# A graph layer on one core: more columns of x[src] on two engines, and their registers loaded eight at a time

## The chip, the core and the metric

One Trainium2 chip, one of its cores. A core has five engines that run their own instruction streams side by side: TensorE (PE; its weight loads are listed as PEld), VectorE (DVE), ScalarE (ACT), GpSimd (POOL) and SyncE (SP, which here only issues transfers). Each engine has a sequencer that takes the instructions in order, does some of them itself (register loads, waits, issuing DMAs) and hands the others on to the engine. The metric is the device time of one execution in microseconds (us), the median of several runs.

## What is computed

A message-passing layer over 12,500 nodes of 64 features and 400,000 edges, sorted by `dst`, with 16 features an edge, followed by a residual and a layer norm. All is float32.

```
m_in = concatenate([x[src], x[dst], edge_attr])      # 400000 x 144
h = silu(m_in @ W1 + b1)
messages = silu(h @ W2 + b2)
agg = segment_sum(messages, dst)                     # 12500 x 64
x = layernorm(x + silu(concatenate([x, agg]) @ W3 + b3))
```

## The kernel before

**Tiles.** 128 edges are a tile, eight tiles an octet; there are 391 octets. Two tiles that lie side by side are a pair (256 edges, four pairs an octet). The loop over octets (`for o in range(NO + 1)`, L601) has a fixed order of instructions on TensorE, ScalarE, VectorE and SyncE (`manual_schedule`, L598): an engine meets its instructions in the order in which the loop body writes them.

**An octet.** `first_layer` (L434) multiplies `xw` (the window's part of the first layer, with the weights of the edge features) by `oh` on L441, and adds the part of `x[src]`. ScalarE takes the silu into `h` (L458). `second_layer` (L461), an octet later, multiplies by W2 (L469), and ScalarE takes the second silu into `m` (L473). `add_up` (L476) sums messages by node with `eh` as a matrix of zeros and ones (L482), and VectorE adds the sums to `agg` (L487). VectorE also builds `oh` by a compare (L424), copies `xw` out of PSUM (L402), and builds `eh` by another compare (L430).

**Where x[src] comes from.** Three ways, side by side:

- *Gathers.* GpSimd issues one indirect DMA a tile (L373), 128 rows of `pa = x @ W1[:64]`, three octets ahead, into one of five tiles `ga`. TensorE adds them through `ident` (L454).
- *Columns.* For some octets the first pair isn't gathered. Instead it is put together, column by column, from `xs`, a copy of x transposed that lies in SBUF. Each edge is one instruction: 64 partitions of 4 bytes are copied from a place given by a register, by ScalarE with a copy (L299), by VectorE with a reduction over one element (L297). TensorE multiplies the finished tile `cx` by `w1d` (L451). The index row of a pair is fetched by SyncE (L351, three octets ahead of the pair's first column), and made into addresses by VectorE (L359).
- *Rows.* Now and then the second pair isn't gathered either: SyncE copies 16 rows an octet, each with a DMA of its own (L324).

**How columns are dealt out.** `columns(o, engine, part)` (L271) is called four times an octet: for VectorE ahead of `first_layer` (L642, behind the compare of L424) and behind `compare_nodes` (L650, behind `xw` and `eh`); for ScalarE ahead of the first silu (L456) and ahead of the second (L471). `ACOLS` and `VCOLS` (L31, L32) say how many columns a call does: 32 and 28 on ScalarE, 32 and 32 on VectorE. `RATE` (L261) is their sum, 124 an octet, so a pair of 256 takes 2.06 octets and there are 182 such pairs. A call works in pieces. Each piece first loads its addresses from the index row into registers (L290, one load instruction for the whole piece), then does its columns. `LOADS` (L34) sets the size of a piece: up to 16 for the first of a call and up to 8 for the others, fewer at the end of a call or where a tile of 128 ends.

Of the kernel before, what the change touches and what calls it, by code (L numbers as in the profile page):

```python
# [20 lines left out]
P = 128  # L21
# [6 lines left out]
AHEAD = 3  # L28
RAW = 12
TABLES = 7  # L30
ACOLS = (32, 28)  # L31
VCOLS = (32, 32)  # L32
ROWS = 16
LOADS = (16, 8)  # L34
XBASE = (0, 64 << 18)
XADDR = 36864
LAG = CT * P // 32
# [60 lines left out]
def windows(ctx, tc, ident, badi, pa, x, xt, src_c, src_row, dst_c, dst_row, attr_t, dst_2, attr_2, base, w1, b1, w2, b2, w3, b3, out, edges):  # L98
    nc = tc.nc
    N, D = x.shape  # L100
# [55 lines left out]
    for s in range(3):  # L156
        part = const.tile([1, D], BF16, name=f"part{s}")
# [90 lines left out]
    with tc.tile_pool(name="gat", bufs=AHEAD + 2) as gat, tc.tile_pool(name="drp", bufs=2) as drp, \  # L248
# [11 lines left out]

        RATE = sum(ACOLS) + sum(VCOLS)  # L261
        pairs = []
        while True:
            o = RAW + -(-2 * P * (len(pairs) + 1) // RATE) + 1
# [3 lines left out]
        cols, indices = {}, {}  # L268
        xb = xs.bitcast(U8)

        def columns(o, eng, part):  # L271
            if o < RAW:
                return
            lo = (o - RAW) * RATE
            if eng == ENG.Activation:
                lo, n = lo + sum(ACOLS[:part]), ACOLS[part]
            else:
                lo, n = lo + sum(ACOLS) + sum(VCOLS[:part]), VCOLS[part]
            hi, todo = lo + n, n
            while lo < hi:  # L280
                j, e0 = lo // (2 * P), lo % (2 * P)
                if j >= len(pairs):
                    return
                n = min(hi - lo, P - e0 % P, LOADS[lo > hi - todo])
                if pairs[j] not in cols:
                    cols[pairs[j]] = cx.tile([P, P], F32, name="cx")
                t = cols[pairs[j]].bitcast(U8)
                s = e0 // P
                h = slice(s * D, (s + 1) * D)
                _, regs = nc.values_load_multi_w_load_instructions(  # L290
                    indices[j][0:1, e0:e0 + n], engines=(eng,), min_val=XBASE[s] + XADDR,
                    max_val=XBASE[s] + XADDR + 4 * (N - 1), skip_runtime_bounds_check_because="src names a node")
                for e, r in zip(range(e0 % P, e0 % P + n), regs):
                    to, frm = t[h, 4 * e:4 * e + 4], xb[h, ds(r - (XBASE[s] + XADDR), 4)]
                    if eng == ENG.DVE:

                        nc.vector.tensor_reduce(to, frm[:, :, None], AX.X, OP.max)  # L297
                    else:
                        nc.scalar.copy(to, frm)  # L299
                lo += n  # L300


        rpairs = []
        while True:
            o = RAW + -(-2 * P * (len(rpairs) + 1) // ROWS) + 1
# [128 lines left out]
        def first_layer(o):  # L434
            c, t0, n, first, last = octs[o]
            n2 = n + n % 2
            k = n2 // 2
            ga = got.pop(o)
            oh, eh = hots.pop(o)
            p1 = ps1.tile([P, OT // 2, P], F32, name="p1")  # L440
            nc.tensor.matmul(p1[:, :k], xw[o % 3], oh, start=True, stop=False, skip_group_check=True)  # L441
            if o < RAW:
                pt = mis.tile([P, OT // 2, P], F32, name="mm")
                for i in range(k):
                    nc.tensor.matmul(pt[:, i, :], ga[:, 2 * i:2 * i + 2, :].rearrange("p s d -> p (s d)"), ident,  # L445
                                     start=True, stop=True)
                xg = work.tile([P, OT // 2, P], F32, name="m")
                nc.vector.tensor_copy(xg[:, :k], pt[:, :k])
                nc.tensor.matmul(p1[:, :k], w1d, xg[:, :k], start=False, stop=True, skip_group_check=True)
            if o in pairs:  # L450
                nc.tensor.matmul(p1[:, 0, :], w1d, cols.pop(o), start=False, stop=False, skip_group_check=True)  # L451
            for i in range(1 if o in pairs else 0, k if o >= RAW else 0):
                g2 = single.pop(o) if o in rpairs and i == 1 else ga[:, 2 * i:2 * i + 2, :]
                nc.tensor.matmul(p1[:, i, :], g2.rearrange("p s d -> p (s d)"), ident,  # L454
                                 start=False, stop=(i == k - 1), skip_group_check=True)
            columns(o, ENG.Activation, 0)  # L456
            h = work.tile([P, OT // 2, P], F32, name="h")
            nc.scalar.activation(h[:, :k], p1[:, :k], AF.Silu, bias=b1s)  # L458
            made[o] = h, eh

        def second_layer(o):  # L461
            c, t0, n, first, last = octs[o]
            n2 = n + n % 2
            k = n2 // 2
            h, eh = made.pop(o)
            p2 = ps2.tile([P, OT, D], F32, name="p2")
            nc.tensor.matmul(p2[:, :n2, :], one3, b2r[:, :n2, :], start=True, stop=False, skip_group_check=True)  # L467
            for i in range(k):
                nc.tensor.matmul(p2[:, 2 * i:2 * i + 2, :].rearrange("p s d -> p (s d)"), h[:, i, :], w2d,  # L469
                                 start=False, stop=(i == k - 1), skip_group_check=True)  # L470
            columns(o + 1, ENG.Activation, 1)  # L471
            m = work.tile([P, OT, D], F32, name="m")
            nc.scalar.activation(m[:, :n2], p2[:, :n2], AF.Silu)  # L473
            made[o] = m, eh
# [85 lines left out]
        todo = {}  # L560
# [7 lines left out]
        for q in range(early):  # L568
            o = lead[due[q]] + 3 if q < rest else NO
# [4 lines left out]
        for q0, q1 in batches:  # L574
            o = lead[due[q1 - 1]] + 3
# [22 lines left out]
        with tc.manual_schedule(engines={ENG.PE, ENG.Activation, ENG.DVE, ENG.SP}):  # L598
            compare_dst(0)
            compare_nodes(0)  # L600
            for o in range(NO + 1):  # L601
# [3 lines left out]
                for k in parts[3 * o - 3:3 * o] if o else []:  # L605
                    n = min(XC, NP - k)
# [33 lines left out]
                if o + 1 < NO:  # L640
                    compare_dst(o + 1)
                columns(o, ENG.DVE, 0)  # L642
                if o < NO:
                    first_layer(o)
# [10 lines left out]
                if 30 <= o < 30 + 2 * LP and o % 2 == 0:  # L655
                    k = (o - 30) // 2
                    part = rel[:, k * TILES // LP:(k + 1) * TILES // LP]
# [307 lines left out]
```

## Time and profile before

| What | Number |
|---|---|
| time, median of 3 runs | 5,184.74 us (5,167.56 to 5,185.11) |
| the profiled execution | 5,200.1 us, of which the span is 5,197.9 us |
| TensorE busy | 2,932.5 us (56%) |
| VectorE busy | 2,641.3 us (51%) |
| ScalarE busy | 2,906.1 us (56%) |
| GpSimd busy | 2,565.3 us (49%) |
| mean granted clock of TensorE | 0.629 |
| a column on VectorE (L297) | 150 ns, 24,032 times |
| a column on ScalarE (L299) | 188 ns, 22,560 times |
| a gather (L373) | 944 ns, 2,619 times from `pa` |
| compare `oh` (L424), `eh` (L430), copy `xw` (L402) | 674, 545, 282 ns |
| silu `h` (L458), silu `m` (L473) | 684, 593 ns |

No engine is busy much over half of the span. The busy shares are flat over the span from its third slice of 40 on, so that one octet is like another: 5,198 us over 391 octets are 13.3 us each. The durations of consecutive columns overlap, so a run of them takes less than their number times the mean. Register loads are done by the sequencer and count as idle time of the engine; so does a wait that the profile can't put down to another instruction, which it calls "issue". A letter q behind an engine's name marks what its sequencer does.

### The profile page before, as it was taken

How to read it: one execution, taken by the hardware profiler on the slowest of the kernel's cores; microseconds unless marked ns; L12 is line 12 of the kernel's file. 1: busy time of each engine (PE TensorE's matmuls, PEld its weight loads, DVE VectorE, ACT ScalarE, POOL GpSimd, SP SyncE). 2: the span in 40 equal slices, each digit the busy share in tenths (PEclk: the TensorE clock that was granted, in tenths of full speed). 3: DMA queues.
4: the chain of work that ended last, by engine and by line, in shares of the span. 5: the costliest groups of instructions: out<-in, count | busy, mean ns of one | idle time of the engine just before them, and what ended most of it. 6: DMA issues, size and time to landing. Idle time of an engine off the chain costs nothing. (4 is left out here: it accounts for less than half of the span.)

```text
span 5197.9 us, 107486 instructions
## 1 busy us (share of the span) xinstructions
PE 2932.5 (56%) x15131; PEld 2075.4 (40%) x15131; DVE 2641.3 (51%) x26395; ACT 2906.1 (56%) x23402; POOL 2565.3 (49%) x2724
## 2 busy tenths in 40 slices
PE   5655655555555555555564655656555555555566
PEld 3443434434433344343343434434433343344344
DVE  1255555545555555555555555555555555555555
ACT  1255555555555655655556565555556555655555
POOL 5544454454444544445444444545454444555453
PEclk7666565666666666666656566565656666665656
DMA  4321111211211121122112211211211221121121
GB/s 85 86 46 39 40 39 40 47 39 40 46 42 43 40 46 40 40 43 42 41 40 49 43 40 42 44 39 40 47 40 40 44 47 40 40 47 39 40 46 40
DMA packets 203943, 229.98 MB, mean 44 GB/s; under 512 B 133612, under 2 KB 141988, under 8 KB 202324
## 3 DMA queue, kind: packets, MB, share of 16 engines
q1 hardware_dynamic: 101528, 122.61, 10.5%
q0 software_dynamic: 86880, 89.14, 9.1%
q10 hardware_dynamic: 14812, 11.26, 0.9%
q14 instruction: 595, 4.87, 0.3%
q8 instruction: 128, 2.10, 0.2%
HBM read 216.36 MB, written 6.40 MB: 43 GB/s over the span
## 5 line engine op out<-in xcount | busy, mean ns | idle before, releaser
L373 POOL DMA_INDIRECT ga<-pa,sc x2619 | 2472.2, 944 | 2516.1 <-PE p L454 1699.8
L299 ACT COPY cx<-xs 64x4 uint8 x22560 | 2404.2, 188 | 1406.1 <-issue 1362.4
L297 DVE TENSOR_REDUCE cx<-xs 64x4 uint8 x24032 | 1910.3, 150 | 1806.6 <-issue 1740.9
L441 PE MATMUL p<-oh,xw 128*128 128x512 f32 (+1 forms) x782 | 772.4, 1089 | 1529.3 <-DVE xw L402 727.6
L441 PEld LDWEIGHTS p<-oh,xw 128*128 128x128 f32 x782 | 187.1, 297 | 1637.1 <-DVE xw L402 776.3
L482 PE MATMUL pg<-eh,m 128*64 128x48 f32 x6250 | 363.0, 277 | 588.6 <-ACT m L473 174.1
L454 PEld LDWEIGHTS p<-ident,ga 128*128 128x128 f32 x2620 | 591.3, 314 | 194.9 <-issue 193.6
L469 PE MATMUL p<-w2d,h 128*128 128x128 f32 x3126 | 642.0, 369 | 1.5 <-issue 1.4
L469 PEld LDWEIGHTS p<-w2d,h 128*128 128x128 f32 x3126 | 545.3, 263 | 133.0 <-issue 133.0
L454 PE MATMUL p<-ident,ga 128*128 128x128 f32 x2620 | 593.2, 397 | 0.0
L482 PEld LDWEIGHTS pg<-eh,m 128*64 128x64 f32 x6250 | 312.1, 189 | 680.2 <-issue 342.2
L473 ACT ACTIVATE m<-p 128x512 f32<-128x512 f32 x391 | 231.8, 593 | 474.9 <-remote 308.9
L458 ACT ACTIVATE h<-p,b1s 128x512 f32<-128x512 f32 x391 | 267.4, 684 | 319.0 <-remote 138.6
L402 DVE TENSOR_TENSOR xw<-mm,mask 96x128 f32<-96x128 f32 x391 | 110.4, 282 | 439.9 <-issue 392.4
L397 PE MATMUL mm<-w1bb,xr 64*96 64x128 f32 x782 | 241.0, 401 | 72.6 <-ACT z L523 49.9
L424 DVE TENSOR_TENSOR oh<-dr,wrow 96x512 f32<-96x512 int32 x391 | 263.6, 674 | 6.3 <-issue 3.5
L430 DVE TENSOR_TENSOR eh<-wrow,dc 128x384 f32<-128x384 f32 x391 | 213.2, 545 | 42.2 <-issue 42.2
L467 PE MATMUL p<-b2r,one 3*128 3x512 bf16 x391 | 194.5, 498 | 0.0
L451 PEld LDWEIGHTS p<-cx,w1d 128*128 128x128 f32 x364 | 116.0, 319 | 175.4 <-issue 175.4
L397 PEld LDWEIGHTS mm<-w1bb,xr 64*96 64x96 f32 x782 | 127.8, 214 | 144.7 <-issue 68.7
L487 DVE TENSOR_TENSOR agg<-agg,pg 128x48 f32 x391 | 77.3, 198 | 123.4 <-remote 32.3
L373 POOL DMA_INDIRECT ga<-in_x,sc x96 | 91.0, 948 | 63.5 <-PE mm L445 28.9
(81 smaller groups left out, 802.7 us busy)
## 6 DMA issues: line engine op xcount, KB each, us to landing
rx<-pa SPq DMA_DIRECT2D x5888, 0.2 KB
dr<-in_dst SPq DMA_DIRECT2D x260, 288.0 KB
ga<-pa,sc POOLq DMA_INDIRECT x2619
oh<-in_attr SPq DMA_DIRECT2D x130, 192.0 KB
xr<-in_xt SPq DMA_DIRECT2D x391, 24.0 KB
xs<-in_xt ACTq DMA_DIRECT2D x12, 512.0 KB
pa<-v ACTq DMA_DIRECT2D x12, 256.0 KB
xa<-in_x SPq DMA_DIRECT2D x24, 128.0 KB
```

Source lines behind the costliest of these rows:

```text
L297: nc.vector.tensor_reduce(to, frm[:, :, None], AX.X, OP.max)
L299: nc.scalar.copy(to, frm)
L373: nc.gpsimd.indirect_dma_start(out=ga[:, i, :], out_offset=None, in_=x if o < RAW else pa[:, :], in_offset=bass.IndirectOffsetOnAxis(ap=sc ...
L397: nc.tensor.matmul(pw[:E, :], winrow[o].rearrange("k s w -> k (s w)"), w1bb.rearrange("k s m -> k (s m)"), start=True, stop=True)
L424: nc.vector.tensor_tensor(oh[:E, :], dr[:, e:e + w], wn[:E, o:o + 1].to_broadcast([E, w]), op=OP.is_equal)
L430: nc.vector.tensor_tensor(eh[:, :n], row[:, None, :].to_broadcast([P, n, S]), rel[:, t0:t0 + n, None].to_broadcast([P, n, S]), op=OP.is_equal)
L441: nc.tensor.matmul(p1[:, :k], xw[o % 3], oh, start=True, stop=False, skip_group_check=True)
L454: nc.tensor.matmul(p1[:, i, :], g2.rearrange("p s d -> p (s d)"), ident, start=False, stop=(i == k - 1), skip_group_check=True)
L458: nc.scalar.activation(h[:, :k], p1[:, :k], AF.Silu, bias=b1s)
L469: nc.tensor.matmul(p2[:, 2 * i:2 * i + 2, :].rearrange("p s d -> p (s d)"), h[:, i, :], w2d, start=False, stop=(i == k - 1), skip_group_ch ...
L473: nc.scalar.activation(m[:, :n2], p2[:, :n2], AF.Silu)
L482: nc.tensor.matmul(pg[s * D:(s + 1) * D, :], m[:, i, :], eh[:, i, :], start=(i < 2), stop=(i >= n - 2), skip_group_check=True)
```

## The change

Each of the two engines does 68 columns an octet: 36 in the first call and 32 in the second. `RATE` becomes 136, a pair takes 1.88 octets, and there are 199 pairs by columns. Every piece has at most eight columns, the first of a call too. `columns` is cut into three functions: `pieces` yields the sizes, `addresses` loads the registers, `columns` calls both. The loads stay where they were in the order of each engine: right ahead of the columns that use them. The calls of `columns` are the same four, at the same places.

```diff
-ACOLS = (32, 28)
-VCOLS = (32, 32)
+ACOLS = (36, 32)
+VCOLS = (36, 32)
 ROWS = 16
-LOADS = (16, 8)
+LOADS = 8
...
-        def columns(o, eng, part):
+        def pieces(o, eng, part):
...
-            hi, todo = lo + n, n
+            hi = lo + n
             while lo < hi:
                 j, e0 = lo // (2 * P), lo % (2 * P)
                 if j >= len(pairs):
                     return
-                n = min(hi - lo, P - e0 % P, LOADS[lo > hi - todo])
+                n = min(hi - lo, P - e0 % P, LOADS)
+                yield j, e0, n
+                lo += n
+
+        def addresses(eng, j, e0, n):
+            s = e0 // P
+            _, regs = nc.values_load_multi_w_load_instructions(
+                indices[j][0:1, e0:e0 + n], engines=(eng,), min_val=XBASE[s] + XADDR,
+                max_val=XBASE[s] + XADDR + 4 * (N - 1), skip_runtime_bounds_check_because="src names a node")
+            return regs
+
+        def columns(o, eng, part):
+            for j, e0, n in pieces(o, eng, part):
+                regs = addresses(eng, j, e0, n)
                 if pairs[j] not in cols:
                     cols[pairs[j]] = cx.tile([P, P], F32, name="cx")
                 t = cols[pairs[j]].bitcast(U8)
                 s = e0 // P
                 h = slice(s * D, (s + 1) * D)
-                _, regs = nc.values_load_multi_w_load_instructions(
...
                 for e, r in zip(range(e0 % P, e0 % P + n), regs):
...
-                lo += n
```

More of the change, by code (lines that the diff above doesn't have):

```diff
@@ L289, in columns @@
                 h = slice(s * D, (s + 1) * D)
-                _, regs = nc.values_load_multi_w_load_instructions(
-                    indices[j][0:1, e0:e0 + n], engines=(eng,), min_val=XBASE[s] + XADDR,
-                    max_val=XBASE[s] + XADDR + 4 * (N - 1), skip_runtime_bounds_check_because="src names a node")
                 for e, r in zip(range(e0 % P, e0 % P + n), regs):
```

## The prediction

> **What bounds the kernel now.** I read the table of groups first, to see which engine is idle for lack of data and which for other reasons; then the waits, for who waits for whom; then the timeline of single octets, for what the idle time of VectorE is made of.
>
> From the groups of the page, and from the waits:
>
> ```profile
> L373 POOL DMA_INDIRECT ga<-pa,sc x2619 | 2472.2, 944 | 2516.1 <-PE p L454 1699.8
> L299 ACT COPY cx<-xs 64x4 uint8 x22560 | 2404.2, 188 | 1406.1 <-issue 1362.4
> L297 DVE TENSOR_REDUCE cx<-xs 64x4 uint8 x24032 | 1910.3, 150 | 1806.6 <-issue 1740.9
> ...
> PE p L441 <- DVE xw L402: 727.6, 160, 9.5
> ...
> DVE xw L402 <- issue: 392.4, 151, 6.3
> DVE m L448 <- remote: 44.2, 3, 32.5
> ```
>
> GpSimd isn't the bound: it stands 1,699.8 us waiting until TensorE has read a gather tile. TensorE waits for VectorE's `xw`. VectorE waits for almost nobody: 1,740.9 us of its idle time stand before columns and 392.4 before `xw`, both "issue", time in which the profile shows nothing to wait for. The next largest entry is 44.2 us, in the first octets. 2,641.3 us busy and some 2,200 us of issue make 4,840 of 5,197.9 us. VectorE's own instruction stream sets the pace, and the question is what its issue time is.
>
> Two things, by the timeline. Loads of registers, first over the span, then in a 1.8 us window that holds the starts of two consecutive loads of VectorE:
>
> ```profile
> L290 DVEq TENSOR_LOAD <-cxi x2391: 340/597/1340, 221.4 to 5159.0; - x200
> L290 ACTq TENSOR_LOAD <-cxi x2352: 305/547/1255, 222.9 to 5158.7; - x196
> ...
> L290 DVEq TENSOR_LOAD <-cxi x2: 594/844/1095, 2611.2 to 2612.8; - x2
> ...
> 300.41 0.62 DVE L297 TENSOR_REDUCE cx<-xs 64x4 uint8 x8 [0.24 <-issue]
> 301.33 0.62 DVE L297 TENSOR_REDUCE cx<-xs 64x4 uint8 x8 [0.30 <-issue]
> ```
>
> (The columns of the L290 rows are least, median and greatest ns.) A load is executed by the sequencer, which can't hand on columns meanwhile. The load of sixteen takes 1,095 ns, that of eight 594. From the start of the load of sixteen to the next load pass 1.66 us (2611.18 to 2612.84, unrounded): load and sixteen columns. Eight columns with their load take 0.92 us (300.41 to 301.33), of which the engine works 0.62 and then idles 0.30. So the sequencer, not the engine, is what is full.
>
> The second thing: stretches in which VectorE and ScalarE both go one column in 0.71 us.
>
> ```profile
> 2617.44 0.15 DVE L297 TENSOR_REDUCE cx<-xs 64x4 uint8 x1 [0.53 <-issue]
> 2618.16 0.15 DVE L297 TENSOR_REDUCE cx<-xs 64x4 uint8 x1 [0.57 <-issue]
> 2618.87 0.15 DVE L297 TENSOR_REDUCE cx<-xs 64x4 uint8 x1 [0.56 <-issue]
> ...
> 2617.44 0.19 ACT L299 COPY cx<-xs 64x4 uint8 x1 [0.46 <-issue]
> 2618.16 0.19 ACT L299 COPY cx<-xs 64x4 uint8 x1 [0.53 <-issue]
> ```
>
> SyncE is issuing its row transfers then, and GpSimd a burst of gathers. Along the timeline I count 1,909 us of such stretches, 5 us of a 13.1 us octet. What causes them I can't say; they come mostly where both of those queues are active, and neither belongs to column work. One stretch (2615.5 to 2624.0) holds 19 columns of VectorE in 8.5 us; the 7.6 us ahead of it hold 64.
>
> **The change part by part.**
>
> *Columns.* At its sizes the loop puts 25,444 columns on VectorE (24,032 so far) and 25,500 on ScalarE (22,560): 199 pairs come from columns, where there were 182.
>
> *Loads on VectorE.* Before: 682 of sixteen, 1,525 of eight, 161 of four, 23 of twelve, together the row's 2,391. After: 2,993 of eight and 375 of four, 3,368. With the turns from above, 1.66 us for sixteen and 0.92 for eight (so 0.0925 a column and 0.18 fixed: 1.29 for twelve, 0.55 for four), the sequencer needs 1,132 + 1,403 + 89 + 30 = 2,653 us before and 2,754 + 206 = 2,960 after: **+307 us**. A column rises from 110 to 116 ns: the fixed part is paid more often.
>
> Here a rule speaks. The Trainium skill, "DMA: Bandwidth & Descriptors", section "Latency and other measured facts", gives `tensor_load` a floor of about 600 ns and says that the compiler unrolls by four to spread it. With a floor alone 977 more loads would cost 586 us. The rows show no such floor (340 ns at the least, the loads of four; 594 and 1,095 for eight and sixteen), but a fixed part and a slope. The loads alone, without the columns behind them, then grow by some 180 us. I take the rows; the rule's direction, that splitting loads costs, agrees.
>
> *What part of it shows.* The slow stretches have a pace of their own: 1,909 us by 19/8.5 columns per us are some 4,270 columns, 18%, that the turns don't set. For the rest, 19,762 by 0.1104 before and 21,174 by 0.1163 after: **+281 us**. Nothing hides it: VectorE waits for nobody, and `xw`, for which TensorE waits, stands in the stream behind the first part of the columns.
>
> *The order.* "None ahead" changes nothing: before, too, each load stands in the stream where its columns do. The first load of sixteen runs while the engine still does the compare (674 ns) or `eh` (545); its overhang is the 0.2 us idle before a first run of columns. A load of eight hides there whole, but the next one is then due after eight columns, 0.5 us of engine work against 0.6 of load. The gain returns as a gap a moment later, since the sequencer stays full. Bounds: nothing gained, or 0.25 us in each of 750 parts; I take nothing, as the 0.30 us gap after eight columns is in the trace.
>
> *ScalarE.* 2,940 more copies of 0.094 us (32 in 3.09 us) are 275 us of engine work; a load of eight (547 ns) hides behind eight copies (0.75 us). ScalarE has some 600 us of waiting for TensorE ahead of its two silus (308.9, 138.6, 100.8 and smaller ones), so this fits. If it didn't, the end would be about the same 275 us later, not that on top.
>
> *Gathers.* 17 pairs are 34 gathers fewer, of 0.944 + 0.30 us: 42 us. Between 0 (GpSimd waits for TensorE anyway) and 42, as octets with fewer gathers have shorter slow stretches; I take 42.
>
> *Index rows.* 17 more index loads on SyncE, and 34 multiplications on VectorE of 220 ns, +7 us. A pair's three index buffers are held longer relative to their 1.88 octets (2.06 before); SyncE waits for them 17.1 us in all so far. It loads three octets ahead, so another wait of a few us a pair stays covered; without cover the rows and windows behind it on SyncE would be late.
>
> Sum: 281 - 42 + 7 = **+246 us**, or 4.7% of the 5,197.9 us span (5,200.1 with what lies around it). On the median of the runs, 5,184.7 us, that is **5,430 us**. Its own range is 5,330 to 5,540: the slow columns' share and the gathers between their ends, and the two engines' lateness adding up now and then.
>
> **The rivals.**
>
> *The slow stretches grow with time.* If they are a share of time, not a number of us an octet, the added 307 us are stretched by 1/(1 - 1,909/5,198): 485 - 42 + 7 = +450, **5,635 us**. For it: they occur all along the span. Against it: rows and gathers of an octet stay as many.
>
> *The engine's pace counts, not the sequencer's.* Then 1,412 columns of 0.063 us (16 in 1.10 us) cost 89 us, less 42: **5,232 us**. For it: 24 columns run in 1.69 us without a gap after `eh`. Against it: the gap after nearly every later run.
>
> *Faster: the overhang of the load of sixteen was the stall.* If a load of eight stayed covered everywhere, 750 overhangs of 0.25 us would go, -188 + 89 - 42 = -141: **5,044 us**. It decides where eight columns last longer than their load; 0.50 against 0.59 us says that they don't on VectorE, though on ScalarE they do.
>
> *No change*: that the added turns fall into waits which the profile lists as issue.
>
> **How the numbers follow.** 62% for the forecast, 10% for growing stretches, 13% for the engine's pace, 9% for faster, 6% for no change. This kernel's runs can tell 0.5% (26 us). Slower by more: 62 + 10 + 13 = 85%; within: 6%; faster: 9%. The range of 5,225 to 5,600 leaves out the last two and half of the growing stretches, 20%.
>
> **What would show it.** The register loads of VectorE should be about 3,368, nearly all of 597 ns. The issue time before columns on VectorE should rise by some 150 us or more, in gaps of 0.3 us after runs of eight, and runs of 24 should be gone. TensorE's wait for `xw` should grow, and GpSimd's for TensorE too. I am wrong on the mechanism if VectorE's issue time stays, or if ScalarE's waits for TensorE vanish instead (then ScalarE is the bound), and wrong on the size if the slow stretches grow much beyond 1,909 us.

## The result and the profile after

| | before | after |
|---|---|---|
| median of 4 runs | 5,184.92 us | 5,427.86 us |
| lowest to highest | 5,167.56 to 5,191.62 | 5,423.18 to 5,434.05 |
| span of the profiled execution | 5,197.9 us | 5,432.3 us |
| VectorE busy | 2,641.3 us | 2,796.6 us |
| ScalarE busy | 2,906.1 us | 3,234.0 us |
| GpSimd busy | 2,565.3 us | 2,535.3 us |

The ratio is 1.0475, interval 1.0447 to 1.0503: slower by 4.7%. Of the four sessions of experiments below, the last gave 3,435.7 us for the very same kernel before, so each ratio here is taken against the kernel before of its own session.

From the groups of the page after, and from its waits (the line numbers have moved: gathers are L382, columns L307 and L309, `xw` L411):

```profile
L382 POOL DMA_INDIRECT ga<-pa,sc x2585 | 2442.4, 945 | 2784.2 <-PE p L463 2059.9
L309 ACT COPY cx<-xs 64x4 uint8 x25500 | 2739.9, 188 | 1416.2 <-issue 1363.4
L307 DVE TENSOR_REDUCE cx<-xs 64x4 uint8 x25444 | 2071.9, 148 | 1817.0 <-issue 1748.0
...
PE p L450 <- DVE xw L411: 1390.2, 234, 9.7
DVE xw L411 <- issue: 481.3, 226, 6.6
```

TensorE's wait for `xw` has nearly doubled (727.6 us before), and GpSimd waits 360 us more for TensorE: the octet has become longer on VectorE, and the others stand by. The issue time before VectorE's columns has hardly changed (1,740.9 before). What has grown on VectorE is its busy time, by 155 us, and the issue time before `xw`, by 89 us (392.4 before).

The register loads of the changed kernel over the span, and one part of its columns in the timeline of VectorE; below them, such a part in the profile of before:

```profile
L290 DVEq TENSOR_LOAD <-cxi x3368: 339/596/853, 220.8 to 5386.5; - x199
...
2608.01 0.68 DVE L433 TENSOR_TENSOR oh<-dr,wrow 96x512 f32<-96x512 int32 x1
2608.72 0.62 DVE L307 TENSOR_REDUCE cx<-xs 64x4 uint8 x8
2609.57 0.62 DVE L307 TENSOR_REDUCE cx<-xs 64x4 uint8 x8 [0.23 <-issue]
2610.50 0.62 DVE L307 TENSOR_REDUCE cx<-xs 64x4 uint8 x8 [0.30 <-issue]
2611.42 1.02 DVE L307 TENSOR_REDUCE cx<-xs 64x4 uint8 x12 [0.30 <-issue]
2612.72 0.29 DVE L411 TENSOR_TENSOR xw<-mm,mask 96x128 f32<-96x128 f32 x1 [0.28 <-issue]
...
2611.47 0.68 DVE L424 TENSOR_TENSOR oh<-dr,wrow 96x512 f32<-96x512 int32 x1
2612.36 1.78 DVE L297 TENSOR_REDUCE cx<-xs 64x4 uint8 x24 [0.21 <-issue]
2614.52 0.60 DVE L297 TENSOR_REDUCE cx<-xs 64x4 uint8 x8 [0.38 <-issue]
2615.04 0.27 DVE L402 TENSOR_TENSOR xw<-mm,mask 96x128 f32<-96x128 f32 x1
```

The first eight follow the compare without a gap: their load is over before the compare is. The later eights start 0.85 to 0.93 us apart. From the compare to `xw` pass 4.71 us for 36 columns, and 3.57 us for 32 in the octet of before. These two octets lie further apart than most. Over all octets in which this part holds nothing but columns and lies outside the slow stretches (counted here as from 4 us after the first gather of a burst, that is of gathers less than 1.6 us apart, to 1 us after its last), the medians are 4.53 us (18 octets) and 3.82 us (70). The turns of the prediction give 4.23 and 3.50 us, nearly the same difference. Runs of 24 columns without a gap, which the prediction expected to go, fell from 133 to 18.

### The profile page after: what moved, and what is told of

It reads as the page before. It is cut to its first block, busy times and chain, and to the rows that moved or that the text cites. A ratio compares the mean times of both kernels' runs of the same rounds, so it can differ in the third digit from the quotient of the medians.

```text
span 5432.3 us, 114104 instructions
## 1 busy us (share of the span) xinstructions
PE 2910.2 (54%) x15131; PEld 2055.6 (38%) x15131; DVE 2796.6 (51%) x27841; ACT 3234.0 (60%) x26342; POOL 2535.3 (47%) x2690
## 5 line engine op out<-in xcount | busy, mean ns | idle before, releaser
L382 POOL DMA_INDIRECT ga<-pa,sc x2585 | 2442.4, 945 | 2784.2 <-PE p L463 2059.9
L309 ACT COPY cx<-xs 64x4 uint8 x25500 | 2739.9, 188 | 1416.2 <-issue 1363.4
L307 DVE TENSOR_REDUCE cx<-xs 64x4 uint8 x25444 | 2071.9, 148 | 1817.0 <-issue 1748.0
L450 PE MATMUL p<-oh,xw 128*128 128x512 f32 (+1 forms) x782 | 793.5, 1117 | 2034.9 <-DVE xw L411 1390.2
L478 PE MATMUL p<-w2d,h 128*128 128x128 f32 x3126 | 606.8, 353 | 1.1 <-issue 1.1
L478 PEld LDWEIGHTS p<-w2d,h 128*128 128x128 f32 x3126 | 513.7, 249 | 125.2 <-issue 125.2
L411 DVE TENSOR_TENSOR xw<-mm,mask 96x128 f32<-96x128 f32 x391 | 110.8, 283 | 523.6 <-issue 481.3
L460 PEld LDWEIGHTS p<-cx,w1d 128*128 128x128 f32 x398 | 132.1, 332 | 202.2 <-issue 202.2
L460 PE MATMUL p<-cx,w1d 128*128 128x128 f32 x398 | 124.7, 416 | 0.0
```

What stands on the lines that cost most here:

```text
L382: nc.gpsimd.indirect_dma_start(out=ga[:, i, :], out_offset=None, in_=x if o < RAW else pa[:, :], in_offset=bass.IndirectOffsetOnAxis(ap=sc ...
```

## The experiments

**The two halves of the change, each alone.** First the columns without the splitting, as an edit of the changed kernel.

```diff
-LOADS = 8
+LOADS = (16, 8)
...
-            hi = lo + n
+            hi, todo = lo + n, n
...
-                n = min(hi - lo, P - e0 % P, LOADS)
+                n = min(hi - lo, P - e0 % P, LOADS[lo > hi - todo])
```

> The changed kernel with the first piece of each call back at up to sixteen columns: 68 columns an octet on each engine, 2,666 loads on VectorE where the change has 3,368. Theory (VectorE's sequencer is full; a turn costs 0.18 us and 0.0925 us a column): VectorE's turns take 2,833 us against 2,653 before and 2,960 after, so after the same discounts about 130 us over before, 5,315 us, half of the loss gone. Rival (the engine's pace counts, the size of loads is indifferent): like the change, 5,430 us. Rival (the slow stretches carry the loss and follow the number of columns, not of loads): also near 5,430 us, with slow stretches as long as after.

5,358.74 us, 1.0292 (1.0221 to 1.0364) of the 5,198.26 us of its session: 160 us over before by the medians, 152 by the ratio (115 to 189). That is over half of the loss, in line with the theory's 130 us given this interval, and well under the change's 243: the size of loads matters, but less than half.

Then the splitting without the columns.

```diff
-LOADS = (16, 8)
+LOADS = (8, 8)
```

> The kernel before with pieces of up to eight alone: 60 and 64 columns, 3,096 loads on VectorE where before has 2,391, the same columns and gathers. Theory (full sequencer): VectorE's turns take 2,780 us against 2,653, so some 115 us over before, 5,300 us. Rival (the first load of sixteen was the stall): faster than before, by up to 190 us. Rival (only columns cost): no change, 5,185 us.

5,252.08 us, 1.0115 (1.0084 to 1.0146): 54 us by the medians, 60 by the ratio (44 to 76), about half of what the turns said. Neither rival holds: it is slower, and it is not nothing. The group of VectorE's columns and its wait before `xw` show where the time went:

```profile
L297 DVE TENSOR_REDUCE cx<-xs 64x4 uint8 x24032 | 1957.6, 148 | 1783.0 <-issue 1688.6 <-remote 25.4 <-ACT h L458 2.4
...
DVE xw L402 <- issue: 466.0, 198, 5.6
```

For the same 24,032 columns the issue time is 52 us less than before; that fits an overhang of the load of sixteen behind the compare, which is gone. The busy time is 47 us more (1,910.3 before). Columns that follow closely start 64 ns apart, while the last of a run shows its whole 150 ns; the trace has 4,509 runs where before had 3,930, and 579 by 86 ns are 50 us. The issue time before `xw` is 74 us more (392.4 before). Together these are +69 us, near the measured 54 to 60. So the price of the many short runs stands under "busy" and before `xw`, where I hadn't looked for it.

**One engine at a time.**

```diff
-VCOLS = (32, 32)
+VCOLS = (36, 32)
...
-                n = min(hi - lo, P - e0 % P, LOADS[lo > hi - todo])
+                n = min(hi - lo, P - e0 % P, LOADS[eng == ENG.DVE or lo > hi - todo])
```

> VectorE alone changed: 68 columns in pieces of eight on VectorE, ScalarE stays at 60 with its first sixteen; 188 pairs by columns. Theory (VectorE's sequencer is the bound): its turns are 2,974 us against 2,653, so about 280 us over before after the discounts, 5,465 us, as slow as the whole change or slower, since fewer gathers go. Rival (ScalarE's columns carry the loss): within 1% of before.

5,415.28 us, 1.0439 (1.0416 to 1.0462) of 5,186.59 us: 229 of the 243 us of the whole change, with ScalarE untouched.

```diff
-ACOLS = (32, 28)
+ACOLS = (36, 32)
...
-                n = min(hi - lo, P - e0 % P, LOADS[lo > hi - todo])
+                n = min(hi - lo, P - e0 % P, LOADS[eng == ENG.Activation or lo > hi - todo])
```

> ScalarE alone changed: 68 columns in pieces of eight on ScalarE, VectorE stays at 64 with its first sixteen; 193 pairs by columns. Theory (VectorE is the bound, ScalarE's 275 us more of copies go into its waits for TensorE): VectorE's turns are 2,644 us as before, so no change or up to 27 us faster for 22 gathers less, 5,160 to 5,200 us. Rival (ScalarE is the bound, or the two add up because TensorE waits for both in turn): 100 to 250 us slower, 5,285 to 5,435 us.

5,293.46 us, 1.0212 (1.0181 to 1.0243): 107 us slower, the low end of the rival. The waits of the two kernels, VectorE's alone first, then ScalarE's:

```profile
PE p L441 <- DVE xw L402: 1468.9, 246, 9.8
ACT m L473 <- remote: 1170.2, 239, 25.5
```

```profile
PE pg L482 <- ACT m L473: 969.9, 190, 16.6
```

With more work on VectorE alone, TensorE waits for `xw` and ScalarE waits as well, for 1,170 us ahead of `m` (the profile doesn't say for whom; "remote" is a releaser that it can't name). With more on ScalarE alone, TensorE waits for `m` instead (174.1 us before), and its wait for `xw` falls to 41.0 us in the groups. So before the change the two streams were nearly level: either, lengthened, takes the lead. In the changed kernel both are longer, and VectorE is the later one: TensorE's matmuls wait 1,390.2 us for `xw` and only 31.5 us for `m`. The two losses don't add.

**How far the price of a turn carries.**

```diff
-LOADS = (16, 8)
+LOADS = (32, 32)
```

> The kernel before with one load for all columns of a call (up to 32), the same 60 and 64 columns. Theory (a turn costs 0.18 us and 0.0925 us a column, and the sequencer is full): 912 loads on VectorE, turns of 2,387 us against 2,653, so about 245 us faster, 4,940 us. Rival (a long load leaves the engine idle[...]; the engine's idle time is what counts): a load of 32 takes 2.1 us[...] 1.3 us idle in each call, so slower than before by up to 300 us.

5,156.44 us, 0.994 (0.9914 to 0.9965): 0.6% faster, an eighth of what the theory says, though the rival's loss isn't there either. The load of 32 and one part of the columns:

```profile
L290 DVEq TENSOR_LOAD <-cxi x912: 341/2099/2376, 217.9 to 5107.7; - x183
...
2629.78 0.67 DVE L424 TENSOR_TENSOR oh<-dr,wrow 96x512 f32<-96x512 int32 x1
2631.34 2.12 DVE L297 TENSOR_REDUCE cx<-xs 64x4 uint8 x32 [0.89 <-issue]
2633.39 0.27 DVE L402 TENSOR_TENSOR xw<-mm,mask 96x128 f32<-96x128 f32 x1
```

From the compare to `xw` pass 3.61 us for 32 columns; the median outside the slow stretches is 3.92 us, against 3.82 with pieces of 16, 8 and 8. The engine idles 0.89 us until the long load is over and then works through all 32 at its own pace; sequencer and engine take turns instead of overlapping. The linear price of a turn (0.18 us and 0.0925 us a column) fits eight, twelve and sixteen: from load to load the medians are 0.92, 1.31 and 1.67 us in the trace of before, outside the slow stretches. It is a little low for four (0.63 us against 0.55), and it doesn't hold at 32.

The edit changes ScalarE too, whose long loads take 1,728 ns, and it became nearly as late as VectorE:

```profile
PE p L441 <- DVE xw L402: 465.0, 114, 9.4
PE pg L482 <- ACT m L473: 416.0, 130, 14.2
```

Before, these waits were 727.6 and 174.1 us. How much of the missing gain is ScalarE's wasn't tried apart.

**The row transfers.** 

```diff
-ROWS = 16
+ROWS = 0
...
-        while True:
+        while ROWS:
```

> The kernel before with ROWS at 0: SyncE issues no row transfers, the 23 pairs they filled are gathered (46 gathers more). Theory (slow stretches need SyncE's row transfers beside GpSimd's gathers): the stretches at 0.71 us a column go nearly whole, VectorE then takes about 8 us an octet and GpSimd 7.0 gathers of 1.25 us, 8.8 us, so about 9.5 us an octet and 3,700 to 4,200 us in all. Rival (the stretches come from the gathers alone): they stay, and the time is 5,185 us within 2%, or up to 60 us more for the gathers.

> The changed kernel with ROWS at 0. Theory (full sequencer, and slow stretches that need the rows): without slow stretches the whole 307 us of added turns show against the kernel before without rows, or less where GpSimd sets the pace there (34 gathers fewer would then make it up to 40 us faster). Rival (the loss of the change is growth of the slow stretches, which rows cause): without rows the two kernels agree within 1%.

5,015.46 us, 0.9631 (0.9564 to 0.9699), and for the changed kernel without rows 5,220.42 us, 1.0028 (1.0007 to 1.0049). The rows cost 3.7%, not a fifth, and my theory of the slow stretches fails: in the timeline of the kernel without rows VectorE still steps at 0.71 us:

```profile
2603.32 0.15 DVE L297 TENSOR_REDUCE cx<-xs 64x4 uint8 x1 [1.17 <-issue]
2604.03 0.15 DVE L297 TENSOR_REDUCE cx<-xs 64x4 uint8 x1 [0.56 <-issue]
2604.74 1.35 DVE L297 TENSOR_REDUCE cx<-xs 64x4 uint8 x17 [0.56 <-issue]
```

The stretches are there without SyncE's row transfers, so these don't make them. The change costs nearly as much without rows: 205 us, a ratio of 1.041 between the two medians, so its loss isn't tied to rows either.

I then counted VectorE's columns by the time since a burst of gathers began, averaged over all bursts of a trace:

| columns a us | first 3.5 us | 4.5 to 8.5 us | from burst to burst |
|---|---|---|---|
| before | 7.6 | 1.4 | 13.2 us |
| after | 7.4 | 1.6 | 13.8 us |
| before without rows | 7.6 | 1.9 | 12.7 us |
| after without rows | 7.3 | 1.7 | 13.3 us |

The stretches sit behind the third gather of a burst and end about 1 us after its last, in all four, and are nearly the same before and after. What the change adds stands outside them.

**Pauses between gathers**, to try that reading.

```diff
+                if o >= RAW and i in (2, 5):
+                    nc.gpsimd.iota(pause, pattern=[[1, 393]], base=0, channel_multiplier=0)
```

> The kernel before, in which GpSimd also writes a scratch tile (an iota of 393 numbers, 1.2 us in the profile of before) behind the third and the sixth tile of an octet, so that no more than three gathers follow one another. In the profile of before VectorE does 7 to 9 columns a us in the first 3.5 us of a burst of gathers and 0.6 to 2.6 from 4.5 us to its end. Theory (the slow stretches come from a burst's gathers behind the third, not from the row transfers): they shrink by half or more, an octet loses 2.5 us or more, 4,250 us or less; GpSimd has 4.4 us of idle time an octet for 3 us of pauses. Rival (they follow GpSimd's activity as such, or time): the column rate falls at the same moments, and the time is 5,185 us or up to 500 us more.

5,544.6 us, 1.0502 (1.046 to 1.0543) of 5,280.62 us. It decides nothing. GpSimd's order isn't the hand-written one, and the writes of the scratch tile were all put ahead:

```profile
L379 POOL IOTA pause<- x734: 457/458/538, 79.8 to 696.0; 128x393 int32 x184
```

All 734 lie in the first 700 us; the bursts behind them have no pause. The loss lies there too: VectorE's sum of the 40th octet starts at 913 us, where it starts at 647 us in the profile of before. So I made the pause part of the data.

```diff
+            k = 0
...
+                k += 1
+                if o >= RAW and k % 3 == 0 and i + 1 < n:
+                    nc.gpsimd.tensor_copy(ga[:, i + 1:n, :], ga[:, i:i + 1, :].to_broadcast([P, n - i - 1, D]))
```

> The kernel before, in which GpSimd copies the third gathered tile of an octet (and the sixth) over the places of the tiles still to be gathered, which the gathers then overwrite: so the next gather waits for the landing of the third, some 2 us after its issue, and for the copy, and no more than three gathers follow one another. Theory (a burst's gathers behind the third make the slow stretches): VectorE's columns stay at 5 or more a us through the burst, an octet loses 2.5 us or more, 4,300 us or less. Rival (the stretches follow GpSimd's activity or some fixed time, whatever the spacing): the column rate falls at the same moments, and the time is 5,185 us or up to 500 us more.

4,730.73 us, against 3,435.7 us for the kernel before in that session: 1.3772 (1.3749 to 1.3795). VectorE's columns do keep their pace, but here the kernel before seems to have run without its slow stretches too (it was 1,750 us faster than in the other sessions; it has no trace there), so the pause had little left to remove. The row transfers in the trace of the kernel with pauses, and two of its waits:

```profile
L324 SPq DMA_DIRECT2D rx<-pa x5888: 224/228/380, 141.1 to 4563.4; - x197
...
POOL ga L379 <- DMA ga<-pa,sc: 1019.0, 554, 4.8
DVE cx L297 <- issue: 511.2, 1512, 1.0
```

No row transfer takes more than 380 ns (up to 1,406 in the first profile), and VectorE's issue time is 511 us where it was 1,741. What the pause costs is GpSimd's own time, 1,019 us of waiting for landings, and GpSimd's gathers are the bound: TensorE waits 1,586.6 us for them to land.

**Other shares of columns.** No columns, no rows (`COLUMNS` is false; the rows are switched off as above):

```diff
+COLUMNS = False
...
-        while True:
+        while COLUMNS:
```

> The kernel before without columns and without rows: every tile of x[src] is gathered by GpSimd. Theory (columns are what fills VectorE; what they save of gathers is worth less): GpSimd sets the pace with eight gathers of 1.25 us an octet, 10.0 us, 3,910 us and some 200 us for the first octets, 4,050 to 4,200 us. Rival (bursts of eight gathers slow all engines' sequencers, columns or not): 5,000 us or more.

4,658.03 us, 0.898 (0.8963 to 0.8997) of 5,186.59 us: faster than both kernels, though not by as much as GpSimd's 1.25 us a gather allows. VectorE and ScalarE have next to nothing to do and still wait on the way:

```profile
L488 DVE TENSOR_TENSOR agg<-agg,pg 128x48 f32 x391 | 80.0, 205 | 3129.2 <-remote 2531.4
...
L374 POOL DMA_INDIRECT ga<-pa,sc x3029 | 2860.8, 944 | 1592.9 <-issue 809.0
```

Most of these waits are "remote", so why this kernel misses the theory's 4,050 to 4,200 us stays open.

Then half the columns, without rows:

```diff
-ACOLS = (32, 28)
-VCOLS = (32, 32)
+ACOLS = (16, 16)
+VCOLS = (16, 16)
```

> 16 and 16 columns an octet on each engine, each call with one load of sixteen, no rows: 64 columns an octet, a pair by columns each fourth octet, 7.5 gathers an octet. Theory (VectorE is full with 64 columns of its own; GpSimd's gathers bound the kernel without columns): 32 columns take VectorE 3.3 us of turns and 5 us of slow stretch, 9.5 to 10 us an octet with the rest, GpSimd 9.4 us; so 4,000 to 4,500 us, below the 4,658 us of no columns. Rival (the bursts hold up the other engines' sequencers, and columns add to what waits there): between no columns and 64 a engine, 4,700 to 5,000 us.

4,577.76 us, 0.8673 (0.8636 to 0.8709) of 5,280.62 us: the fastest in a session with slow stretches, above the theory's 4,500 and below the rival's 4,700. With the pause behind the fourth gather added to it, in the last session:

> The kernel with 16 and 16 columns on each engine and no rows, with the same pause behind the fourth gather of an octet. Theory (bursts of more than three or four gathers hold up the other engines): VectorE's and ScalarE's waits shrink, GpSimd needs 9.4 + 2 us an octet; 4,300 to 4,550 us against 4,578. Rival (spacing is indifferent, and GpSimd has no idle time to give): 2 us an octet more, up to 5,300 us.

4,492.46 us, 1.3085 (1.3063 to 1.3107) of that session's 3,435.7 us. It says nothing on bursts, for the same reason: 7.5 gathers of 1.25 us and 2.0 us of pause are 11.4 us an octet of GpSimd's time, and 391 of them 4,450 us, near the measured time.

## Why the prediction was right, point by point

The forecast was 5,430 us; measured are 5,427.86.

*What bounds.* VectorE's stream: held. Changed alone it brings 229 of 243 us. That ScalarE's stream was almost as late, the prediction didn't see.

*The loads on VectorE.* The count is right to the one (3,368), and so is a turn of 0.92 us. But the term was mis-sized: the splitting alone costs 54 to 60 us where 127 us of turns stood for it, 104 after the prediction's discount for slow columns (the experiment's "some 115" was itself too high). I had kept the overhang of the load of sixteen at nothing; the 52 us of issue time that went in the experiment with eights alone are about what is missing.

*The columns.* 152 to 160 us. The prediction's turns, gathers and index rows, redone without the splitting, give 141, within the interval of 115 to 189. The halves add to some 212 us and the whole is 243. The 30 us between lie within what the intervals allow, so whether the two act on each other isn't shown. That the sum came within 3 us of the measured time is in part luck: the splitting was put 45 us too high, and the halves as measured fall 30 us short of the whole.

*The rise of issue time.* I expected 150 us or more before columns on VectorE and had written that I'd be wrong on the mechanism if it stayed. It rose by 7. VectorE's time did grow, by 155 us of busy and 79 of idle; of the columns' 162 us more, 1,412 columns of 0.063 us explain 89, and the rest is what shorter runs share less (843 more runs by 86 ns are 72 us). Of the idle time, 89 us stand before `xw`. By its own words this sign speaks against the mechanism; what speaks for it are the turns of 0.92 us and the part ahead of `xw`, which is longer by the 0.7 us that the turns say. The test was badly chosen: a turn is full whether the profile calls its parts busy or idle.

*ScalarE.* Right for the sum, wrong in its reason. I held its 275 us of copies to be covered by 600 us of waits for TensorE. The two largest of these, 308.9 and 138.6 us, are "remote" in the profile and not TensorE's. Alone the copies cost 107 us, so the waits didn't cover them. In the change they are hidden because VectorE is later still.

*Gathers and index rows.* Neither was tried alone; 42 us less and 7 us more stay argued. GpSimd's wait for TensorE grew by 360 us, so little can have come from its 34 gathers directly.

*The slow stretches.* They didn't grow. Steps of 0.6 to 0.8 us from one column to the next add up to more than before (878 us against 780 on VectorE, 1,130 against 940 on ScalarE), which looks like the rival. But the stretches themselves, from 4 us after the first gather of a burst to 1 us after its last, take 1,981 us where they took 2,023, and hold 2,887 of VectorE's columns where they held 2,881. So the prediction's 4,270 slow columns, read off one stretch with 19 in 8.5 us, were too many, and the discount too large; with 2,881 the turns give some 290 us in place of 281. That they come mostly where SyncE's rows are active says nothing of their cause: they are there without rows too.

*Faster.* The overhang seems real and worth about 50 us, not 188; it was never enough against 0.3 us behind each later eight.

## What to carry to other kernels

When two engines feed a third in turn and neither waits much, lengthening either costs time, and lengthening both costs about the larger; a wait in the profile is slack only if an experiment says so. For instructions that take their address from a register, count what the sequencer does between two of them: small loads pay their fixed part more often and large ones leave the engine idle. Here the choice was worth little: eights alone were 1.2% slower than sixteen and eights, and loads of 32 were 0.6% faster. A sum that comes out right may hold a term that is wrong, which only the halves of the change, each run alone, bring to light.

## What the runs showed of the hardware that wasn't expected

In three sessions, and in the runs of the result, VectorE, ScalarE and SyncE often went one instruction in some 0.71 us during bursts of gathers, from some 4 us after the start of a burst until about 1 us after its last gather, with or without row transfers. In the last session there was next to nothing of it: VectorE's steps of 0.6 to 0.8 us add up to 32 us in the trace with pauses and to 21 us with half the columns, and the kernel before took 3,435.7 us, some 1,750 us less than in the others, nearly as much as the 1,909 us that the prediction counted. GpSimd's gathers were issued every 1.25 us in either case, and their last packet ended some 2.1 us after their issue. The cause isn't settled. Transfers of instructions (queue q14 of the profile) take as long inside the stretches of before as outside, 486 and 479 ns, so slow fetching doesn't show. That it went away with the same kernel says that the program alone doesn't make it, and the session before ran on the same chip. Whether the change is slower where the stretches are missing wasn't tried: there 6.9 gathers of 1.25 us are 8.6 of the 8.8 us an octet, so GpSimd may be the bound and the added columns partly hidden. Half the columns is the better choice where the stretches occur; where they don't, 7.5 gathers of 1.25 us an octet are an estimated 3,670 us, over the 3,435.7 us of the kernel before, but it wasn't run there without pauses.
